# Moving turned softmax squares inside SBUF with twelve small DMAs instead of through DRAM, with a key ring whose last half is repeated

## The chip, the cores and the metric

The kernel runs on one core of a Trainium2 chip. The metric is the device time of one execution in microseconds, as the median over several runs. Beside it there is one profiled execution, whose trace gives the views that this document reads.

## The reference

Input x has 2 batches of 2048 tokens with 128 features, all in float32. There are three parts, with layer norms and residual additions between them. The whole is computed as follows:

```
y = norm(x);  x += softmax(y y^T over the first token axis) y        # once, 2048 x 2048 per batch
twice:
    s = norm(x)
    for each of 2 layers:                                             # 8 heads of 64, window 64
        h = half of the features of s shifted by one token
        q, k, v = h @ wqkv;  q, k = rotate(l2norm(q)), rotate(l2norm(k))
        p = softmax of q k^T over the own window of 64 keys and the one before
        s = s + (p v) @ wo
        s = s + (a * gelu(g)) @ w2,   a, g = norm(shifted s) @ w1     # hidden 341
    x += s
    after the first of the two: x += a token-wise weighting of norm(x)
```

The part that matters here is the windowed attention. For a query u of a group of 32 queries, the keys that count are 96 keys in three squares of 32: the weights of a group and head are a 32 x 96 matrix. To multiply the weights with the values, they must be turned so that keys lie on partitions.

## The kernel before

The kernel keeps activations transposed, features on partitions and tokens along the row. Tokens are cut into blocks of 128 (`NBLK` = 16 per batch) and chunks of 512. The first attention is one stage per batch (`first_attention`, L439 on). After it come four passes (two repetitions of two batches), each of 16 blocks through two layers: layer 1 runs `LAG` = 6 blocks behind layer 0, and the end of one pass runs beside the start of the next. In all there are 128 calls of `Attention.block`, which begins near L543.

The order of the work is not written by hand. Each step is declared with `op(engine, cost, fn, r, w, claim, late)`; `Program.run` is a list scheduler that knows each step's cost and the time until its result can be used (`TAIL`, `tail`), gives out buffers from pools (`slots`), and takes on each engine the ready step with the smallest number plus `late`. A step may start only if its buffers are free and the steps ahead of it can still be given theirs (`room`). What comes out is a fixed order on each of the five queues: TensorE (PE), VectorE (DVE), ScalarE (ACT), GpSimd (POOL) and SyncE (SP), which issues all DMAs. Each queue runs strictly in that order.

One block of windowed attention takes these steps, with the lines of the profile:

- A DMA fetches the rotation table (L551). TensorE projects q and k (L559, two steps) and v (L566); ScalarE squares (L582) and copies v (L567); two DMAs shift v by 64 partitions (L569, L573).
- VectorE multiplies with the table (L583, L584), reduces the squares (L587), and with a small matmul (L588) and POOL's products (L591, L597) q and k are normalised.
- VectorE turns q (L606) and k (L607). The turned keys go to `kring`, a ring of `R` = 3 slots of 128 keys per layer.
- TensorE computes the scores (L628), with masks added by matmuls (L637). `keys(a)` says where the 96 keys of a group of 32 queries lie in the ring; on slot 0 the keys of the block before are at the ring's other end, so groups 0 and 1 take two pieces.
- VectorE takes the maximum (L649), ScalarE the exponentials (L654), VectorE the sum and its reciprocal (L660, L661), POOL multiplies (L666).
- VectorE turns the weights in squares of 32 x 32 (L677) into `xp`. Four DMAs write the rows of `xp` to a DRAM buffer `far`, one for each group (L686), and one DMA reads the whole back as `pT` with all four groups beside each other (L691). The parts of `far` that no square covers were set to zero once, by 32 DMAs (L520).
- TensorE combines values and weights (L702), ScalarE copies the result (L709), and every second block TensorE applies `wo` (L715). Every fourth block is followed by the feed-forward part (L751, L767, L776).

Buffers of 128 x 1024 floats come from the pool `w`. At the start it is empty: its 18 parts are first the buffers of the first attention and turn into `w` when that has done with them. `xn0` and `xnT0` are free when batch 0 has passed the first attention, the others when batch 1 has.

## Time and profile before

| what | value |
|---|---|
| median of 3 runs | 1640.41 us (1636.79 to 1644.73) |
| the profiled execution | 1623.37 us, of which its span is 1621.3 us |
| granted TensorE clock, mean | 0.96 |
| busy: PE, DVE, POOL, ACT | 91%, 83%, 66%, 59% of the span |
| DMAs issued by SP | 1164 |
| moved by the DMA engines | 208.55 MB |

A busy share counts the time in which at least one instruction of the engine ran. PEld is TensorE's loading of weights, which runs beside its matmuls. SP counts no busy time: its instructions issue DMAs or wait. In the rows, `out<-in` names the tile written and the tile read; `far` is the DRAM buffer, while `arena` and `right` are the memory from which the pool `w` is made.

### The profile page before, as it was taken

Reading aid. Unit: us, or ns where it says so; the run is one execution under the profiler, and the core shown is the slowest. Engines: PE = TensorE matmul, PEld = TensorE weight load, DVE = VectorE, ACT = ScalarE, POOL = GpSimd, SP = SyncE. Lnnn points to the kernel's source line nnn. Section 1 sums busy time; section 2 is a strip of 40 time slices with the busy share of each in tenths; the row PEclk is TensorE's granted clock in tenths of the full one; section 3 lists DMA queues with packets and bytes.
Section 4 is the critical chain, followed back from the end, with each engine's and each line's share of the span. In section 5 each row is a group of like instructions: output and inputs, shape, how many; then the busy total and the mean of one; then the engine's idle time right before and its main releaser. Section 6 shows DMA issues by size and latency. Waiting matters only on the chain.

```text
span 1621.3 us, 53049 instructions
## 1 busy us (share of the span) xinstructions
PE 1482.7 (91%) x21659; PEld 844.0 (52%) x21659; DVE 1341.4 (83%) x2464; ACT 960.0 (59%) x2426; POOL 1072.2 (66%) x1308
## 2 busy tenths in 40 slices
PE   7999997989999999699999899799999999899875
PEld 4454554545555555355555464455555555555543
DVE  4533378799999899989998999989999989899772
ACT  6453455566666566465666666556666756566652
POOL 3440147578697767758687757758697877786561
PEclk9999998999999999799999999789999999999997
DMA  5540025455464543235555443255555555555432
GB/s 191 163 148 1 14 67 142 111 150 156 136 172 124 156 134 97 84 98 167 144 144 164 118 137 105 58 153 152 147 153 169 154 147 157 139 152 153 133 97 60
DMA packets 183542, 208.55 MB, mean 129 GB/s; under 512 B 18474, under 2 KB 143876, under 8 KB 183300
## 3 DMA queue, kind: packets, MB, share of 16 engines
q1 hardware_dynamic: 183300, 205.18, 44.4%
q8 instruction: 170, 2.79, 0.7%
q14 instruction: 72, 0.59, 0.1%
HBM read 111.78 MB, written 61.87 MB: 107 GB/s over the span
## 4 chain that ended last, share of the span: by engine, by line
PE 60%; DVE 17%; DMA 9%; POOL 5%; issue 4%; SPq 2%; ACT 2%; POOLq 0%; DVEq 0%; ACTq 0%
PE pp L751 9%; PE pp L559 9%; PE pp L702 6%; PE pp L628 6%; PE pp L715 5%; PE pp L468 5%; PE pp L566 5%; PE pp L776 4%; DMA arena<-far 3%; PE pp L482 2%; PE pp L479 2%; PE pp L460 2%; DMA right<-far 2%; DVE b_m L660 2%; DMA far<-arena 2%
## 5 line engine op out<-in xcount | busy, mean ns | idle before, releaser
L559 PE MATMUL pp<-wqkv,b_s 128*32 128x256 f32 x4096 | 263.4, 389 | 3.3 <-DVE arena L584 1.6
L654 ACT ACTIVATE arena<-pp,b_m 128x96 f32<-128x96 f32 x776 | 198.6, 363 | 92.2 <-DVE b_m L649 88.8
L666 POOL TENSOR_TENSOR arena<-arena,b_m 128x384 f32<-128x384 f32 x194 | 156.5, 827 | 91.1 <-DVE b_m L661 47.7
L751 PE MATMUL pp<-b_c,w 128*128 128x512 f32 (+1 forms) x384 | 176.8, 609 | 10.0 <-POOL b_c L747 7.8
L559 PEld LDWEIGHTS pp<-wqkv,b_s 128*32 128x32 f32 x4096 | 115.9, 110 | 129.8 <-issue 29.8
L628 PE MATMUL pp<-kring,b_c 64*32 64x96 f32 (+2 forms) x9728 | 150.2, 245 | 17.5 <-DVE kring L607 8.9
L628 PEld LDWEIGHTS pp<-kring,b_c 64*32 64x32 f32 x9728 | 121.5, 109 | 76.2 <-issue 33.6
L597 POOL TENSOR_TENSOR arena<-arena,b_n 128x1024 f32<-128x1024 f32 x80 | 152.9, 1913 | 3.5
L649 DVE TENSOR_REDUCE b_m<-pp 128x4 f32<-128x384 f32 x256 | 131.2, 540 | 18.8 <-PE pp L637 17.5
L566 PE MATMUL pp<-wqkv,b_s 128*128 128x512 f32 x256 | 143.8, 650 | 2.6 <-DVE b_n L589 2.6
L591 POOL TENSOR_TENSOR arena<-arena 128x1024 f32<-128x1024 f32 x51 | 120.9, 2370 | 36.4 <-DVE arena L584 28.5
L582 ACT ACTIVATE arena<-pp 128x512 f32<-128x512 f32 x170 | 100.9, 605 | 57.7 <-PE pp L559 49.9
L751 PEld LDWEIGHTS pp<-b_c,w 128*128 128x128 f32 (+1 forms) x384 | 67.3, 181 | 104.4 <-issue 72.4
L702 PE MATMUL pp<-arena,b_v 128*64 128x64 f32 x2560 | 96.1, 230 | 25.0 <-DMA arena<-far 14.1
L702 PEld LDWEIGHTS pp<-arena,b_v 128*64 128x64 f32 x2560 | 85.3, 143 | 61.0 <-issue 34.0
L584 DVE TENSOR_TENSOR arena<-pp,b_tab 128x512 f32<-128x512 f32 x172 | 114.0, 673 | 0.2
L583 DVE TENSOR_TENSOR arena<-pp,b_tab 128x512 f32<-128x512 f32 x160 | 105.7, 671 | 9.2 <-ACT arena L582 6.3
L567 ACT COPY b_v<-pp 128x512 f32<-128x512 f32 x128 | 75.7, 594 | 54.0 <-PE pp L566 53.8
L587 DVE TENSOR_REDUCE b_n<-arena 128x32 f32<-128x1024 f32 x85 | 101.8, 1198 | 1.7 <-ACT arena L582 1.7
L709 ACT COPY arena<-pp 128x512 f32<-128x512 f32 x80 | 47.6, 595 | 84.0 <-PE pp L702 82.0
L660 DVE TENSOR_REDUCE b_m<-arena 128x8 f32<-128x768 f32 x97 | 90.5, 933 | 7.3 <-ACT arena L654 6.9
L597 POOL TENSOR_TENSOR right<-right,b_n 128x1024 f32<-128x1024 f32 x48 | 92.3, 1923 | 2.3
(213 smaller groups left out, 3390.5 us busy)
## 6 DMA issues: line engine op xcount, KB each, us to landing
arena<-far SPq DMA_DIRECT2D x80, 512.0 KB, 4.2
far<-arena SPq DMA_DIRECT2D x344, 96.0 KB, 1.9
b_tab<-turn SPq DMA_DIRECT2D x128, 256.0 KB, 3.0
b_v<-b_v SPq DMA_DIRECT2D x248, 128.0 KB, 2.6
right<-far SPq DMA_DIRECT2D x48, 512.0 KB, 4.1
far<-right SPq DMA_DIRECT2D x168, 96.0 KB, 2.5
turn<-b_tab SPq DMA_DIRECT2D x32, 256.0 KB, 2.0
b_tab<-in_rot_dram SPq DMA_DIRECT2D x16, 256.0 KB, 2.8
```

The lines of the kernel that those rows point to most:

```text
L559: pe_.matmul(out=pq[k]()[c * 32 : c * 32 + 32, a * 256 : (a + 1) * 256], lhsT=s()[:, at : at + 32], rhs=wqkv[:, l, c * 256 : (c + 1) * 256 ...
L566: op("PE", 0.885, lambda: pe_.matmul(out=pv(), lhsT=h(), rhs=wqkv[:, l, 2 * INNER : 3 * INNER], start=True, stop=True), r=keys_of(s, q) + ...
L584: op("DVE", dve(512), lambda part3=part3, src=src, trig=trig: dv.tensor_tensor(part3(t2), src(), trig(1), ALU.mult), r=[pq[k], tab], w=[(t ...
L591: op("POOL", pool(1024), lambda: po_.tensor_tensor(halves(t1), halves(t1), halves(t2)[:, :, ::-1, :], ALU.add), r=[t2], w=[t1], late=47)
L597: lambda: po_.tensor_tensor(t1().rearrange("p (h d) -> p h d", d=32), t1().rearrange("p (h d) -> p h d", d=32), nr()[:, 0:32].unsqueeze(2) ...
L628: pe_.matmul(out=sim[par]()[a * 32 : a * 32 + 32, pair * 96 + c0 : pair * 96 + c0 + n], lhsT=qT()[rows, pair * P + a * 32 : pair * P + a * ...
L649: op("DVE", dve(384), lambda sim3=sim3, mx=mx: dv.tensor_reduce(mx(), sim3(), AX.X, ALU.max, negate=True), r=[sim[par]], w=[(nm, par)])
L654: ac.activation(p()[:, hd * 96 : (hd + 1) * 96], sim[par]()[:, k * 96 : (k + 1) * 96], AF.Exp, bias=nm()[:, hd : hd + 1])
L660: op("DVE", dve(768), lambda: dv.tensor_reduce(rs()[:, 0:HEADS], p3(), AX.X, ALU.add), r=[p], w=[rs])
L666: lambda hs=hs: po_.tensor_tensor(p3()[:, hs, :], p3()[:, hs, :], rs()[:, hs].unsqueeze(2).to_broadcast([P, 4, 96]), ALU.mult),
L702: pe_.matmul(out=av()[par * 64 : par * 64 + 64, pair * P + w * WIN : pair * P + (w + 1) * WIN].rearrange("p (a c) -> p a c", a=2), lhsT=(v ...
L751: op("PE", pe(512), lambda: pe_.matmul(out=p_()[0:n, :], lhsT=w1[:, l, off + j * P : off + j * P + n], rhs=d(), start=True, stop=True), r= ...
```

## The change

The squares of the turned weights go from `xp` to `pT` within SBUF: for each of the four groups and each of the three squares one DMA of 32 partitions with 256 floats each, twelve a block, in place of four writes to `far` and one read. `far`, its zeroing DMAs and the constant for them are gone; the uncovered parts of `pT` are zeroed by four memsets on POOL when batch 0's first attention has ended. For this, `pT` has a pool of its own with four buffers, made of `xn0` and `xnT0`, which no longer go to `w`.

The key ring gets 64 more columns in front. When a block has written slot 2, a DMA copies the second half of that slot into them, so that slot 0 finds the keys before it without a break; only the first block of a pass still uses two pieces.

Other pools change in size: `c` 12 to 10, `s1` 3 to 2, `n` 7 to 10, `m` 12 to 18, `row` 4 to 8. The scheduler's figures change: the tail of a DMA from 2.0 to 2.6, the cost of the scores from 1.02 to 1.14 (1.26 for a first block), and nearly every `late` number. So the order on all five queues is a new one. The diff without the `late` numbers:

```diff
-    kring = [fixed([P, 4, R * P], f"kring{l}") for l in range(DEPTH)]
+    kring = [fixed([P, 4, WIN + R * P], f"kring{l}") for l in range(DEPTH)]
...
-    slots["far"] = [scratch.tile([4 * P, 256], F32, name=f"far{i}") for i in range(8)]
+    slots["pT"] = []
...
-        "xn0": [("w", part[4]), ("w", part[5])],
+        "xn0": [("pT", part[4]), ("pT", part[5])],
...
-        "xnT0": [("w", part[8]), ("w", part[9])],
+        "xnT0": [("pT", part[8]), ("pT", part[9])],
...
+        if not b:
+
+            for x in (xn, xnT):
+                for odd in range(2):
+                    z0 = 0 if odd else 96
+                    op("POOL", 1.1, lambda x=x, odd=odd, z0=z0: po_.memset(x()[z0 : z0 + 32, :].rearrange("p (n a c) -> p n a c", n=2, a=4)[:, :, odd::2], 0.0), w=[x])
...
-    def clear():
-        for far in slots["far"]:
-            for a in range(4):
-                z0 = a * P + (0 if a % 2 else 96)
-                op("SP", 0.4, lambda far=far, z0=z0: sp.dma_start(out=far[z0 : z0 + 32, :], in_=I["zero"]), w=[(nought, z0)], late=7)
...
+            if slot == R - 1:
+                op("SP", 0.4, lambda: sp.dma_start(out=ring[:, :, 0:WIN], in_=ring[:, :, R * P : WIN + R * P]), r=[(ring_, slot)], w=[(ring_, "before")], tail=3.0)
...
-                at, own = slot * P + 32 * a - WIN, WIN - 32 * a
+                at, own = slot * P + 32 * a, WIN - 32 * a
                 if own > 0 and first:
-                    return (0, slot * P, own), (own, slot * P, 96 - own)
-                if own > 0 and not slot:
-                    return (0, prev * P + P - own, own), (own, 0, 96 - own)
+                    return (0, WIN + slot * P, own), (own, WIN + slot * P, 96 - own)
                 return ((0, at, 96),)
...
-            xp, pT, far = buf("w"), buf("w"), buf("far")
+            xp, pT = buf("w"), buf("pT")
...
             for a in range(4):
-                op(
-                    "SP", 0.4,
-                    lambda a=a, z0=a * P + 32 * (a % 2): sp.dma_start(
-                        out=far()[z0 : z0 + 96, :].rearrange("(n k) c -> k n c", k=32), in_=xp()[a * 32 : a * 32 + 32, 0:768].rearrange("k (n c) -> k n c", n=3)
-                    ),
-                    r=[xp, nought], w=[(far, a)], tail=3.2, late=85,
-                )
-            op("SP", 0.4, lambda: sp.dma_start(out=pT().rearrange("p (a c) -> p a c", a=4), in_=far().rearrange("(a p) c -> p a c", a=4)), r=[far], w=[pT], tail=3.6, late=40)
+                for n in range(3):
+                    z0 = 32 * (a % 2 + n)
+                    op(
+                        "SP", 0.37,
+                        lambda a=a, n=n, z0=z0: sp.dma_start(out=pT()[z0 : z0 + 32, a * 256 : (a + 1) * 256], in_=xp()[a * 32 : a * 32 + 32, n * 256 : (n + 1) * 256]),
+                        r=[xp], w=[(pT, 3 * a + n)], tail=2.2,
+                    )
```

## The prediction

> **What bounds the kernel now.** I read the page first (engines, slices, chain), then the busy time by stretch, then the score, DMA and wait rows that the change touches.
>
> ```profile
> PE 1482.7 (91%) x21659; PEld 844.0 (52%) x21659; DVE 1341.4 (83%) x2464; ACT 960.0 (59%) x2426; POOL 1072.2 (66%) x1308
> ...
> PE 60%; DVE 17%; DMA 9%; POOL 5%; issue 4%; SPq 2%; ACT 2%; POOLq 0%; DVEq 0%; ACTq 0%
> ```
>
> TensorE holds 60% of the chain that ended last, VectorE 17%. But shares of the whole span mix stages, so I cut it where the first projection of an attention block runs (193.8 us) and where the planner's ramp is over:
>
> ```profile
> 100.00:194.00 94.00, 94.00 (x314) 47.83 (x316) 28.39 (x83) 39.92 (x95) 11.62 (x14) 1.00 0.09 33
> 194.00:221.00 27.00, 27.00 (x272) 14.57 (x265) 20.61 (x41) 13.19 (x29) 12.85 (x14) 1.00 0.23 59
> 221.00:273.00 52.00, 43.78 (x718) 23.95 (x716) 43.42 (x82) 27.86 (x80) 33.14 (x39) 0.95 0.40 107
> ...
> 400.00:650.00 250.00, 239.19 (x3905) 139.03 (x3905) 235.90 (x424) 161.02 (x401) 187.68 (x227) 0.99 0.50 140
> 1060.00:1500.00 440.00, 418.32 (x7319) 243.41 (x7319) 409.73 (x740) 286.15 (x743) 333.38 (x404) 0.98 0.54 152
> ```
>
> The columns after the length are PE, PEld, DVE, ACT, POOL busy. Up to 194 us TensorE is alone at 100% and VectorE at 30%. From 400 us on both are full: PE 95 to 96%, DVE 93 to 94%. So the blocks are bound by two engines at once, and time is gained only if both have less to do or wait less; VectorE has no work to lose in this change.
>
> **Part 1, fewer score matmuls.** With the last half of the key ring repeated in front of it, blocks on slot 0 need no second piece of keys, except the first block of a pass. Slot 0 comes 6 times in 16 blocks, 48 of 128 blocks; 8 of them are first blocks, so 40 change, each losing 16 matmuls. The timeline has both kinds:
>
> ```profile
> 1137.70 1.24 PE L628 MATMUL pp<-kring,b_c 64*32 64x64 f32 x90
> ...
> 1139.06 1.15 PE L702 MATMUL pp<-right,b_v 128*64 128x64 f32 x32
> ...
> 1188.57 0.93 PE L628 MATMUL pp<-kring,b_c 64*32 64x96 f32 x60
> ...
> 1189.60 1.12 PE L479 MATMUL pp<-b_s,meanw 128*128 128x512 f32 x2
> ```
>
> From the first score to the next step: 1.36 us with two pieces, 1.03 us with one. 40 x 0.33 = 13 us of TensorE work go. TensorE has 60% of the chain and VectorE is as full, so I book 8 us of the 13. The 40 added ring copies (one DMA each) follow a transpose whose readers come one block of the same layer later, two block times of 10.6 us (1356 us from 194 to 1550 us over 128 blocks); 3 us of landing fit in. If SP is held up for over 15 us there, the scores wait.
>
> **Part 2, the way of the squares.** The rows of before:
>
> ```profile
> L686 SPq DMA_DIRECT2D far<-arena x344: 302/433/1545, 239.3 to 1587.3; - x172
> L691 SPq DMA_DIRECT2D arena<-far x80: 371/382/1512, 244.2 to 1589.3; - x80
> L573 SPq DMA_DIRECT2D b_v<-b_v x120: 461/590/1724, 198.0 to 1547.4; - x120
> ...
> far<-arena SPq DMA_DIRECT2D x344, 96.0 KB, 1.9
> b_v<-b_v SPq DMA_DIRECT2D x248, 128.0 KB, 2.6
> arena<-far SPq DMA_DIRECT2D x80, 512.0 KB, 4.2
> ```
>
> Issue on SP takes 0.43 us for one of the four writes (0.48 from start to start), and these land 2.1 us later by the median of their line; the read back takes 4.2 us. The path is 3 x 0.48 + 2.1 + 0.2 + 4.2 = 7.9 us a block. No row is an SBUF-to-SBUF DMA of 32 rows of 1 KB. Its issue is bounded by 0.30 (the shortest L686) and 0.64 us from start to start (L573 right behind L569, 0.59 and the gap); I take 0.48, the row with the same kilobyte rows. Landing is bounded by 1.8 and 2.6 us (L569, SBUF to SBUF but four times the bytes); I take 2.1. New path: 11 x 0.48 + 2.1 = 7.4 us, bounds 5.1 to 9.6.
>
> Two rules of the Trainium skill are weighed here. L686 with four writes in 2 us shows that issues follow each other without waiting for landings. "SBUF — State Buffer", The DMA setup-cost knee, says each DMA pays some 2 us whatever its size, and that small ones should be joined; paid one after another this would be 12 x 2 = 24 us a block, a chain of 6.8 + 24 = 31 us against a cover of 17 (both below), and the sum would gain some 14 us on each of 128 blocks. The rows decide: the cost overlaps, and what counts is SP's 0.48. The same page, Door 1: The DMA port swizzle, says that 32 partitions reach 8 of 16 ports, an estimated 0.15 us for 32 KB at its 218 GB/s asymptote; that is below the issue spacing and is left out. Second, "DMA: Bandwidth & Descriptors", Anatomy of one DMA, calls the receipt of a write to HBM the heaviest, so SBUF should land sooner than the far write. The rows show the reverse order, 2.6 against 1.9 us; by the rule the path is at most 7.4 us, by the SBUF row 7.9. Neither changes the sign.
>
> SP's load: before, per block, 4 x 0.48 + 0.43 + 0.42 (table) + 1.15 (two value shifts) = 3.9 us, plus the stops of the queue until the far writes land:
>
> ```profile
> SPq L691 <- DMA far<-arena: 66.1, 71, 4.2
> ```
>
> With the 33.7 us of the same wait on the far writes from the other buffers, 99.8 us of stopped queue go. After: 12 x 0.48 + 0.42 + 1.15 + 0.15 = 7.5 us of every 10.6, 71%. In the changed kernel's order on SP, 64 of the 128 batches of twelve stand alone and the other 64 stand back to back with another batch; the second of a pair may start up to 5.8 us late, and table loads and value shifts queue behind both. In that order each small DMA also waits for the semaphore of the DMA eight before it; at 2.1 us landing and 0.48 spacing only some five are in flight, so this wait ends early; it decides from a landing of 3.8 us.
>
> What covers this path is the TensorE work that the planner put between the scores of a block and its combine. I took both kernels' orders and priced each step by its spacing in the trace (projection half 0.97, values 0.95, combine 1.08, output 1.83, feed-forward 0.89 each and 2.68). Mean cover: before 19.5 us (lowest tenth 15.0), after 16.9 (11.7). What it must cover: first maximum 0.54, eight exponentials 2.9, sum 0.93, reciprocal 0.18, two products 1.65, last transpose 0.56, then the path: 6.8 + 7.9 = 14.7 before, 14.2 after. Adding up the shortfall over all blocks at 14 gives 46 us before; the page's idle time before L702 is 25.0 + 17.6 = 42.6, so the sum is usable. In the middle (TensorE work 300 to 1300 us): before 13.8 us of shortfall at 14; after 7.3 if its chain is 13.5, 28.2 at 15, 55.4 at 16. For the pairs of batches I take 15: +14 us, bounds -7 and +42. At the end of the kernel the shortfall also grows (from 18.5 at 14 us to 48.9 at 15) but the work missing there was done earlier, so I book nothing.
>
> **Part 3, buffers.** Two of the early buffers (xn0, xnT0) now hold pT alone, so the general pool has nothing until the second batch's first attention frees its own. In the order before, the first projection stands 43 us of TensorE work ahead of the last first-attention matmul; after, 6 us. Before, VectorE did 20.6 us in 194 to 221 us, 15.7 of it for blocks by its lines; after, the first projection stands at 208 us of TensorE work, where before it stood at 181 and ran at 194, so it starts at about 221 us. Against that, 5.5 us of first-attention work on VectorE then lies behind it. So VectorE is 10.2 us behind in the stage where it is 93% busy: +11 us. Bounds: 5 (TensorE is free to serve it faster) and 15. If the cover of first-attention matmuls is gone, TensorE idles there; that is the form in which it will show. Four memsets on POOL, an estimated 1.0 us each from the 64x512 one's 0.52, lie where POOL is 12% busy: nothing. The 32 zeroing DMAs (0.59 us each at 35 to 69 us) go from SP, under 100% TensorE: nothing. If POOL or SP were late there, the tables would be, which are read after 194 us.
>
> **Part 4, waits on the engines.** Twelve landings mean more waiting instructions: on TensorE 1021 for 385, 781 of them at the combine for 161; on VectorE 549 for 404. At 51 ns each the 636 on TensorE would be 32 us at most, 7 us on VectorE. Before, a combine with 0, 1 or 2 of them follows an L559 matmul by 522 ns in each case, so they hide behind the matmul ahead; inside a combine one stretched the spacing from 34 to 51 ns. I take 2 us; the cover would fail if three in a row outlast the queue. Moving the remaining steps (new order numbers everywhere) I price at nothing: counts are the same and at each 100 us of TensorE work the VectorE work issued agrees within 5 us.
>
> **Sum.** -8 + 14 + 11 + 2 = +19 us against the profiled execution, which took 1623.4 us with what lies around its span of 1621.3: 1.2%. That execution is 1% below the median of the runs, so I carry the ratio over: 1640.4 x 1.012 = 1659 us.
>
> **Rivals.** Faster (0.26): the removed waits pay and the rest is hidden. L702's waits for the far reads are worth 24.6 us (14.1 + 10.5) on TensorE; half of them go, all 13 us of scores count, and the late start costs its 5: -13 - 12 + 5 = -20, 1620 us. For it: 9% of the chain is DMA, SP is stopped 100 us, the DMA engines lose 512 of 896 rows a block. Against: the planner has spent the shorter path on a thinner cover. It decides from an issue spacing below 0.37 us, where the path falls under 6.2 us and the pairs cost under 4.4.
>
> SP becomes the bound (0.15): at 0.64 us spacing a block costs 9.4 us of SP in 10.6, waits pass from queue to combine (+42 us and more at a chain over 16), and table loads come late: 1690 to 1740 us. Against: L686 shows 0.48.
>
> No change (0.14): early start and scores cancel, stalls in the middle stay as they are: 1640. That the ring does not spare the matmuls is excluded: the order after has 640 fewer.
>
> **Numbers.** About 0.5% (8 us) is what a measurement of this kernel can tell. My case, slower by up to 2.5%, has 0.45; with SP as the bound 0.60 for slower. The range takes in the bounds (-13 + 5 - 7 = -15 to -5 + 15 + 42 + 15 = +67) and part of the faster case: 1614 to 1707 us.
>
> **What would show it.** Right: L628 near 137 us busy instead of 150, first projection near 221 us, TensorE idle 10 us more before 300 us, SP's issues 0.48 apart, waits of the combine for DMA not smaller. Wrong: small DMAs at 0.35 us, PE idle before the combine well under 40 us, or scores waiting for the ring copy.

## The result: 1937 us, and the profile after

The changed kernel takes 1937.24 us (median of 4 runs, 1929.41 to 1939.72); the kernel before, in the same comparison, took 1639.43 us. The ratio is 1.1804, with a 95% interval of 1.1756 to 1.1851. The direction was forecast, the size was not: 298 us instead of 19, far above the range.

First the page of the changed kernel: the engines, and the two rows of the chain that ended last.

```profile
span 1937.9 us, 52332 instructions
...
PE 1596.3 (82%) x20379; PEld 896.4 (46%) x20379; DVE 1341.8 (69%) x2464; ACT 970.9 (50%) x2426; POOL 1076.8 (56%) x1312
...
PE 37%; SPq 28%; DVE 18%; DMA 8%; issue 5%; POOL 2%; ACT 2%; DVEq 0%; POOLq 0%; ACTq 0%
SPq L687 27%; PE pp L467 6%; PE pp L700 5%; DMA arena<-arena 4%; PE pp L749 4%; PE pp L557 4%; PE pp L459 4%; PE pp L564 3%; PE pp L627 2%; PE pp L713 2%; DVE b_m L648 2%; PE pp L774 2%; DMA arena<-right 2%; DVE b_n L585 2%; DVE arena L676 2%
```

No engine is full now. SP's queue had 2% of the chain before; it has 28%, nearly all in line L687, the twelve small DMAs. The trace has 1280 fewer matmuls of TensorE than before (21659; it shows two records for each of the 640 that the new order spares), and yet TensorE is busy 114 us longer. The stretches tell why (columns as before: length, then busy PE, PEld, DVE, ACT, POOL with counts, the granted clock, the DMA share, GB/s):

```profile
194.00:221.00 27.00, 25.93 (x101) 14.17 (x102) 12.70 (x30) 11.51 (x20) 5.25 (x5) 1.00 0.00 1
221.00:273.00 52.00, 42.85 (x637) 22.27 (x635) 43.37 (x79) 24.54 (x68) 29.98 (x33) 0.87 0.21 55
400.00:650.00 250.00, 206.54 (x3050) 117.09 (x3047) 183.33 (x330) 128.47 (x328) 154.00 (x187) 0.90 0.30 79
1060.00:1500.00 440.00, 363.44 (x5092) 205.91 (x5091) 341.81 (x610) 235.66 (x586) 274.54 (x340) 0.91 0.28 74
```

In the middle TensorE is busy 83% (before 95 to 96%) and VectorE 73 to 78% (before 93 to 94%), and the granted clock is 0.90 to 0.91 instead of 0.98 to 0.99. So the loss has two layers: the engines stand, and the matmuls that run take longer. It also runs through all stages; it is no matter of the start.

Now the rows that answer to L686 and to its wait. The first are the answer for line L687 (ns min/median/max, first and last start), then the two landings of the page, then the waits of TensorE (us in total, times, longest), those of the kernel before (L702) last:

```profile
L687 SPq DMA_DIRECT2D arena<-arena x996: 507/589/1967, 257.2 to 1905.0; - x200
L687 SPq DMA_DIRECT2D arena<-right x540: 507/589/2047, 278.5 to 1897.4; - x180
...
arena<-arena SPq DMA_DIRECT2D x996, 32.0 KB, 1.8
...
arena<-right SPq DMA_DIRECT2D x540, 32.0 KB, 1.8
...
PE pp L700 <- DMA arena<-arena: 169.3, 81, 4.4
...
PE pp L700 <- DMA arena<-right: 76.2, 35, 3.7
...
PE pp L702 <- DMA arena<-far: 14.1, 11, 3.1
PE pp L702 <- DMA right<-far: 10.5, 9, 3.9
```

One small DMA holds SP for 0.59 us; from start to start it is 0.633 us by the median in the trace (0.68 us by the mean). Twelve are 7.6 us of issues, and by these medians a batch has landed after 11 x 0.633 + 1.84 = 8.8 us. Landing, 1.84 us by the median, is no slower than the 2.1 us forecast. The combine (L700) now waits 245.5 us for these DMAs; before, its waits for the far reads were 24.6 us. SP's timeline in the middle of the kernel (start, length, what) shows the queue:

```profile
905.39 8.35 SPq L687 DMA_DIRECT2D arena<-right  x12
913.84 0.54 SPq L571 DMA_DIRECT2D b_v<-b_v  x1
914.48 0.54 SPq L567 DMA_DIRECT2D b_v<-b_v  x1
915.11 0.54 SPq L549 DMA_DIRECT2D b_tab<-turn  x1
915.74 8.07 SPq L687 DMA_DIRECT2D arena<-arena  x12
923.91 0.54 SPq L571 DMA_DIRECT2D b_v<-b_v  x1
924.55 9.25 SPq L687 DMA_DIRECT2D arena<-right  x12
```

In this stretch SP waits for nothing. It is not so everywhere: from 300 to 1500 us SP issues for 78% of the time (in the kernel before 39%) and waits in the rest for the steps that its next DMA needs. Everything that an attention block needs from memory goes through this one queue, the rotation tables (L549) and the value shifts (L567, L571) too, so they stand between batches of 8 to 9 us. VectorE now waits for tables, which it does for 1.1 us in all in the kernel `none` below, the same without the small DMAs:

```profile
DVE arena L582 <- DMA b_tab<-turn: 27.7, 7, 11.5
DVE right L582 <- DMA b_tab<-turn: 26.7, 5, 10.7
```

### The profile page after: what moved, and what is told of

Same layout as the page of the kernel before. It is cut to its first block, busy times and chain, and to the rows that moved or that the text cites. A ratio compares the mean times of both kernels' runs of the same rounds, so it can differ in the third digit from the quotient of the medians.

```text
span 1937.9 us, 52332 instructions
## 1 busy us (share of the span) xinstructions
PE 1596.3 (82%) x20379; PEld 896.4 (46%) x20379; DVE 1341.8 (69%) x2464; ACT 970.9 (50%) x2426; POOL 1076.8 (56%) x1312
## 4 chain that ended last, share of the span: by engine, by line
PE 37%; SPq 28%; DVE 18%; DMA 8%; issue 5%; POOL 2%; ACT 2%; DVEq 0%; POOLq 0%; ACTq 0%
SPq L687 27%; PE pp L467 6%; PE pp L700 5%; DMA arena<-arena 4%; PE pp L749 4%; PE pp L557 4%; PE pp L459 4%; PE pp L564 3%; PE pp L627 2%; PE pp L713 2%; DVE b_m L648 2%; PE pp L774 2%; DMA arena<-right 2%; DVE b_n L585 2%; DVE arena L676 2%
## 5 line engine op out<-in xcount | busy, mean ns | idle before, releaser
L700 PE MATMUL pp<-arena,b_v 128*64 128x64 f32 x4096 | 202.8, 254 | 250.3 <-DMA arena<-arena 169.3
L700 PEld LDWEIGHTS pp<-arena,b_v 128*64 128x64 f32 x4096 | 171.3, 162 | 320.5 <-issue 227.2
L665 POOL TENSOR_TENSOR arena<-arena,b_m 128x384 f32<-128x384 f32 x142 | 115.3, 831 | 97.6 <-DVE b_m L660 77.2
L653 ACT ACTIVATE arena<-pp,b_m 128x96 f32<-128x96 f32 x568 | 140.9, 365 | 54.3 <-DVE b_m L648 52.6
L627 PE MATMUL pp<-kring,b_c 64*32 64x96 f32 (+2 forms) x8448 | 142.0, 265 | 24.2 <-DVE kring L605 11.9
L653 ACT ACTIVATE right<-pp,b_m 128x96 f32<-128x96 f32 x456 | 113.3, 358 | 52.7 <-DVE b_m L648 47.6
L582 DVE TENSOR_TENSOR arena<-pp,b_tab 128x512 f32<-128x512 f32 x146 | 96.9, 676 | 56.6 <-DMA b_tab<-turn 27.7
L595 POOL TENSOR_TENSOR arena<-arena,b_n 128x1024 f32<-128x1024 f32 x68 | 130.1, 1913 | 2.5
L665 POOL TENSOR_TENSOR right<-right,b_m 128x384 f32<-128x384 f32 x114 | 92.5, 832 | 65.1 <-DVE b_m L660 46.1
L707 ACT COPY right<-pp 128x512 f32<-128x512 f32 x60 | 35.2, 586 | 183.0 <-PE pp L700 182.5
L589 POOL TENSOR_TENSOR right<-right,arena 128x1024 f32<-128x1024 f32 x34 | 80.3, 2361 | 56.2 <-DVE right L581 52.6
```

The lines of the kernel that those rows point to most:

```text
L582: op("DVE", dve(512), lambda part3=part3, src=src, trig=trig: dv.tensor_tensor(part3(t2), src(), trig(1), ALU.mult), r=[pq[k], tab], w=[(t ...
L595: lambda: po_.tensor_tensor(t1().rearrange("p (h d) -> p h d", d=32), t1().rearrange("p (h d) -> p h d", d=32), nr()[:, 0:32].unsqueeze(2) ...
L627: pe_.matmul(out=sim[par]()[a * 32 : a * 32 + 32, pair * 96 + c0 : pair * 96 + c0 + n], lhsT=qT()[rows, pair * P + a * 32 : pair * P + a * ...
L653: ac.activation(p()[:, hd * 96 : (hd + 1) * 96], sim[par]()[:, k * 96 : (k + 1) * 96], AF.Exp, bias=nm()[:, hd : hd + 1])
L665: lambda hs=hs: po_.tensor_tensor(p3()[:, hs, :], p3()[:, hs, :], rs()[:, hs].unsqueeze(2).to_broadcast([P, 4, 96]), ALU.mult),
L700: pe_.matmul(out=av()[par * 64 : par * 64 + 64, pair * P + w * WIN : pair * P + (w + 1) * WIN].rearrange("p (a c) -> p a c", a=2), lhsT=(v ...
```

## The experiments

Unless it is said otherwise, an experiment has the order and the buffers of the changed kernel, and each time is a median of 4 or 5 runs (narrow: one run; c11: 20). Ratios are to the kernel before, run beside it. Its medians there lie between 1633 and 1643 us, so a difference of under some 10 us between two experiments that were not run beside each other says nothing.

### Was it the order, the work, or the number of small DMAs?

**plan63.** The scheduler is told the measured price, so that the order is planned anew.

```diff
-                        "SP", 0.37,
+                        "SP", 0.633,
```

> The changed kernel, where the planner is told the measured 0.633 us for each of the twelve DMAs instead of 0.37; nothing else. Theory A (the order is wrong: a batch takes 7.6 us on SP where the planner reckoned with 4.4, so TensorE meets each combine some 3 us early and stands still there): the combines are placed later, idle time of TensorE at the combine falls from 250 us to under 80, and the time to 1640 to 1740 us. Theory B (capacity: SP has 9.6 us of issues for every block and cannot serve more blocks, however they are ordered): 1850 us or more, and the waits move elsewhere. Theory C (it is not SP: late start, smaller pools, more waiting instructions): 1900 to 1970 us.

**four.** Of the twelve DMAs only those of the first square of each group are issued; `eight` below issues two of three.

```diff
-  lambda a=a, n=n, z0=z0: sp.dma_start(...)
+  lambda a=a, n=n, z0=z0: (sp.dma_start(...) if n == 0 else None)
```

> The changed kernel with its order kept, but only four of the twelve DMAs of a block are issued, those of the first square of each group; the other squares are left out, so weights of two thirds of the keys are stale. Theories A and B: SP has 4.5 us per block and a batch takes 2.5 us; the time falls to 1620 to 1690 us, what is over 1640 being the price of late start, pools and order. Theory C: the time stays over 1850 us.

plan63 took 1994.42 us, ratio 1.2179 (1.2136 to 1.2222), slower than the changed kernel. Of the three theories only B has room for it (1850 us or more, the waits elsewhere). Its combine waits less for the squares, but the loss has moved to the tables:

```profile
PE pp L700 <- DMA arena<-arena: 56.4, 30, 4.1
PE pp L700 <- DMA arena<-right: 56.0, 32, 3.7
...
DVE arena L582 <- DMA b_tab<-turn: 69.4, 11, 15.8
```

So correcting the cost in the plan wins nothing back. four took 1569.1 us, ratio 0.9578 (0.9547 to 0.9608): with a third of the DMAs, everything else in the change is there and the kernel is 4% faster than before, below the 1620 to 1690 us expected.

**eight** and **narrow** ask for the dose and for the bytes; narrow moves 64 floats a row instead of 256.

```diff
- out=pT()[z0 : z0 + 32, a * 256 : (a + 1) * 256], in_=xp()[a * 32 : a * 32 + 32, n * 256 : (n + 1) * 256]
+ out=pT()[z0 : z0 + 32, a * 256 : a * 256 + 64], in_=xp()[a * 32 : a * 32 + 32, n * 256 : n * 256 + 64]
```

> The changed kernel with its order kept, but eight of the twelve DMAs issued (two squares of each group; the third is left out, so weights of a third of the keys are stale). SP has 7 us per block. If the loss grows evenly with each DMA, half-way between four (1569) and twelve (1937): 1750 us. If it starts only when a batch outlasts the 4.4 us that the order was made for (eight take 5.1), near 1600 us.

> The changed kernel with its order kept, all twelve DMAs issued, each with 64 floats a row instead of 256 (three quarters of each square are left out, so those weights are stale). If the 0.63 us are a price per DMA: spacing and time stay, 1900 to 1940 us. If they are the time of the bytes or of what the DMA engines can take: spacing under 0.4 us and time under 1650 us.

eight took 1655.61 us, ratio 1.0145 (1.0117 to 1.0173). From four to eight DMAs a block, each one more costs 22 us of the whole, from eight to twelve 70 us, so the loss does not grow evenly. narrow took 1893.29 us in its one run, just under the 1900 us expected of a price per DMA. Its issue is unchanged, so a quarter of the bytes takes little away and SP is paid per DMA:

```profile
L687 SPq DMA_DIRECT2D arena<-arena x996: 507/588/1799, 254.9 to 1859.0; - x200
```

### The same load laid on the kernel before

**before_plus8** puts two SBUF-to-SBUF DMAs of 32 rows behind each write to `far`, ahead of the read back, in the old order. **before_8behind** puts eight of 24 floats a row behind the read back, and nobody waits for them.

```diff
                 sp.dma_start(out=far()[z0 : z0 + 96, :]...)                        # before_plus8
+                for j in range(2):
+                    sp.dma_start(out=xp()[b : b + 32, c0 : c0 + P], in_=xp()[a * 32 : a * 32 + 32, j * P : (j + 1) * P])
...
                 sp.dma_start(out=pT()..., in_=far()...)                            # before_8behind
+                for a in range(4):
+                    for j in range(2):
+                        sp.dma_start(out=spare[b : b + 32, j * 24 : (j + 1) * 24], in_=ident[a * 32 : a * 32 + 32, j * 24 : (j + 1) * 24])
```

> The kernel before with its order kept; behind each of the four writes to the DRAM buffer SP issues two more DMAs of 32 partitions from xp into columns of xp that nobody reads, so twelve issues stand ahead of the read back. Theories A and B: 8 x 0.63 = 5 us more on SP in every block, met by a cover of 19.5 us over a chain of 14.7: the chain becomes 19.8, short in nearly half of the blocks, and SP stands at 9 us of 10.6; 1780 to 1950 us. Theory C: within 2% of 1640 us, since eight DMAs that nobody waits for cost only SP's time.

> The kernel before with its order kept; SP issues eight more DMAs of 32 partitions (24 floats a row, between tiles that nobody waits for) directly behind each read back, so the way of the squares itself is as long as before and only SP's time is taken. Theory B1 (SP's time: tables, value shifts and the next batch queue behind): 1800 us or more, near the 2102 of eight DMAs ahead of the read. Theory B2 (the length of the way from scores to combine): within 3% of 1640 us.

before_plus8 took 2102.07 us, ratio 1.2818 (1.2778 to 1.2858), beyond the 1780 to 1950 us expected; before_8behind 1890.01 us, ratio 1.1565 (1.1525 to 1.1604). The second is the cleaner one: SP's time, with no data wanted, costs the old kernel some 250 us. Its combine now waits 151.8 us for its own reads of `far` (before 24.6), which come late. No step reads `spare`, yet the trace puts some waits down to these DMAs too, which is not explained:

```profile
PE pp L710 <- DMA arena<-far: 101.3, 35, 6.6
PE pp L710 <- DMA right<-far: 50.5, 17, 4.9
...
PE pp L710 <- DMA spare<-ident: 34.1, 10, 6.0
```

Laid on the way of the squares, the eight DMAs, here of 128 floats a row and within `xp`, cost another 212 us. Not all of this is the way's length in DMAs: behind DMAs within SBUF the four writes to `far` themselves are issued more slowly, 0.58 us each by the median instead of the 0.43 us of the kernel before:

```profile
L684 SPq DMA_DIRECT2D far<-arena x344: 308/580/1819, 240.8 to 2060.0; - x172
```

So there are two costs, the queue's time and the length of the way, and the next three kernels separate them in the changed order.

### Spacing against waiting

**to_dram** sends the twelve DMAs to DRAM instead of to `pT`.

```diff
- sp.dma_start(out=pT()[z0 : z0 + 32, a * 256 : (a + 1) * 256], in_=...)
+ sp.dma_start(out=out_of(pT(), a, n), in_=...)        # 32 rows of a DRAM scratch, one scratch for each pT buffer
```

> The changed kernel with its order kept; the twelve DMAs go from the same rows of SBUF to a scratch in DRAM instead of to the rows that the combine reads (which stay at zero), so their data are left out, while the combine still waits for all twelve. It asks what sets the 0.63 us from one small DMA to the next, and tests the forecast at its own price. If SBUF on both sides sets it: spacing 0.43 to 0.50 us as for the writes to DRAM of the kernel before, a batch of twelve about 5.8 us, SP at 7.5 us a block, and the time that of about nine DMAs at 0.63 by the counts four, eight and twelve (1569, 1656, 1937): 1690 to 1740 us; by the forecast's sum 1659. If a DMA of 32 rows costs 0.63 us wherever it goes: spacing 0.60 to 0.65 us and 1900 to 1960 us.

One sentence of this expectation was wrong: the combine's matmuls read rows that no DMA writes, so they wait for none of the twelve. What was measured is the spacing alone: 1660.13 us, ratio 1.0153 (1.0117 to 1.019). The issue is short again, 0.464 us from start to start, with landings of 1.6 us:

```profile
L696 SPq DMA_DIRECT2D far<-arena x996: 302/419/1988, 256.6 to 1640.3; - x200
...
far<-arena SPq DMA_DIRECT2D x996, 32.0 KB, 1.6
```

The same source rows, the same 32 x 1 KB; only the destination differs. So it is the destination in SBUF that makes 0.633 us of 0.464; whether that is the memory, or that the rows lie on 32 partitions there and one behind the other in the scratch, is not shown. That 1660 agrees with the forecast of 1659 is chance, since the wait is missing. The next two complete the table: **dram_waits** sends the last of the twelve to `pT`, so that the combine waits for the end of a batch; **nobody** keeps SBUF to SBUF, with 24 floats a row, into a spare tile that nobody reads.

```diff
- out=out_of(pT(), a, n)                                                                     # dram_waits
+ out=pT()[z0 : z0 + 32, a * 256 : (a + 1) * 256] if 3 * a + n == 11 else out_of(pT(), a, n)
...
- out=pT()[z0 : z0 + 32, a * 256 : (a + 1) * 256], in_=xp()[..., n * 256 : (n + 1) * 256]    # nobody
+ out=spare[z0 : z0 + 32, a * 24 : (a + 1) * 24], in_=xp()[..., n * 256 : n * 256 + 24]
```

> In the kernel to_dram no combine waited for a small DMA after all: its matmuls read rows that no DMA wrote. Here eleven of the twelve go to DRAM and the last one to the rows that the combine reads, so the combine waits for the end of the batch (eleven squares are left out). Spacing about 0.48 us on the mean (eleven of 0.46 and one of 0.63), the forecast's own figure, and the way 11 x 0.46 + 1.84 = 6.9 us. If the spacing is the only term of the forecast that failed: 1640 to 1700 us, and 15 to 60 us of waits for DMA at the combine. If waiting for the end of a batch costs by itself what the change lost: 1720 to 1850 us.

> The changed kernel with its order; the twelve small DMAs go from SBUF to a spare tile of SBUF, 24 floats a row, and no engine waits for them; their data are left out. Spacing 0.63 us, as with 64 floats a row, whose time was 1893 us. If SP's time alone is the cost (tables and value shifts late behind 7.6 us of issues): 1780 to 1870 us. If the cost is that the combine waits for the end of a batch of 8.8 us: near to_dram, 1650 to 1700 us.

dram_waits took 1742.2 us, ratio 1.0615 (1.0567 to 1.0663), and nobody 1807.79 us, ratio 1.1014 (1.0959 to 1.1068). In a table, in us:

| spacing of the small DMAs | no combine waits for them | the combine waits |
|---|---|---|
| 0.46 to 0.48 (to DRAM) | 1660 (to_dram) | 1742 (dram_waits) |
| 0.63 (within SBUF) | 1808 (nobody) | 1893 (narrow), 1937 (the changed kernel) |

Going down costs 148 us without the wait and 151 or 195 us with it; going right costs 82 us in the upper row, 85 or 129 in the lower. The columns are not quite alike, since dram_waits waits for the last of the twelve alone and narrow and the changed kernel for all. dram_waits met the expectation of a cost of waiting (1720 to 1850 us), nobody that of a cost of SP's time (1780 to 1870 us); neither alone is the whole. Where the two pay shows in their waits. First dram_waits, then nobody with the issue of its small DMAs; its combine waits for none of them, but its tables and ring copies come late behind them:

```profile
PE pp L709 <- DMA arena<-arena: 82.3, 43, 5.0
PE pp L709 <- DMA arena<-right: 39.6, 23, 4.8
...
L688 SPq DMA_DIRECT2D spare<-arena x996: 507/588/1806, 256.6 to 1800.6; - x200
...
DVE arena L583 <- DMA b_tab<-turn: 73.5, 8, 13.7
...
DVE right L583 <- DMA b_tab<-turn: 59.5, 9, 14.3
...
PE pp L628 <- DMA kring<-kring: 38.5, 8, 15.7
```

In to_dram and nobody the squares are still read from `xp`, whose buffer is free only when they have landed; in nobody waits for that, of ScalarE, GpSimd and VectorE, come to some 64 us in all, none of them at the combine.

### The floors of the two orders

**none** issues no small DMA at all; **before_none** leaves out the four writes and the read back of the kernel before, in its own order, and its combine reads the identity.

```diff
- sp.dma_start(out=pT()...)                                  # none
+ None
...
- sp.dma_start(out=far()...), sp.dma_start(out=pT()..., in_=far()...)   # before_none
+ None
- rhs=pT().rearrange("p (a c) -> p a c", a=4)[:, 2 * w : 2 * w + 2, at : at + 32]
+ rhs=ident[:, at % 64 : at % 64 + 64].rearrange("p (a c) -> p a c", a=2)
```

> The changed kernel with its order and none of the twelve small DMAs; the combine reads rows that stay at zero and waits for no square (the squares are left out). The floor of the changed order: 1540 to 1569 us (four small DMAs gave 1569). Beside before_none it gives the sum of the forecast's parts 1, 3 and 4 without part 2: -8 + 11 + 2 = +5 us by the forecast; if the late start costs nothing, 8 to 13 us less than before_none.

> The kernel before with its order, without the four writes and the read back of each block; the combine's matmuls, same in number and shape, read the identity instead and wait for no square (the squares are left out). The floor of the order before. By the forecast's parts 1, 3 and 4, 5 us less than none; by the matmuls that the repeated ring saves alone, 8 to 13 us more than none. If the two differ by over 25 us, the new order as such is better or worse than the old.

none took 1558.18 us, ratio 0.9514 (0.9452 to 0.9576), and before_none 1591.1 us, ratio 0.9726 (0.9674 to 0.9777). So the way over DRAM cost the old kernel 46 us, the small DMAs cost the new one 379 us, and apart from the way of the squares the changed kernel is 33 us the better. The rows of none to hold against the changed kernel's, and the combine's row in the changed kernel (first) and in none (busy us, mean ns, idle before it):

```profile
PE 1460.8 (94%) x20379; PEld 820.0 (53%) x20379; DVE 1329.5 (85%) x2464; ACT 961.2 (62%) x2426; POOL 1074.1 (69%) x1312
...
400.00:650.00 250.00, 238.17 (x3768) 135.64 (x3774) 239.28 (x431) 167.47 (x416) 197.29 (x243) 0.99 0.21 54
...
L700 PE MATMUL pp<-arena,b_v 128*64 128x64 f32 x4096 | 202.8, 254 | 250.3 <-DMA arena<-arena 169.3
...
L700 PE MATMUL pp<-arena,b_v 128*64 128x64 f32 x4096 | 151.9, 229 | 2.1 <-DVE b_n L587 0.8
```

The matmuls are the same 20379. With the small DMAs they are busy 1596.3 instead of 1460.8 us, 135 us more, at a mean granted clock of 0.90 instead of 0.977; and TensorE stands 1937.9 - 1596.3 = 342 us instead of 98. Thus of 379 us some 244 are standing and 135 slower matmuls. Of the 135, 51 are the combine's alone (202.8 against 151.9 us), whose matmuls are also drawn apart by the waits between them; the other 84 are spread over the other lines. For these the lower clock is the likely cause, and that it follows from the standing is an inference: in the kernels here the clock is lower where TensorE stands more, and the Trainium skill's page "TensorE: Matmul & The Clock Gate", Part 1, says that the gate follows how busy TensorE has just been.

### The order with the old way, and the ring by itself

**far_kept** keeps order and ring of the changed kernel and moves the squares by the old five DMAs, at the places of the twelve. **far_after** does the same with the zeroing and the buffers of before as well, and is planned anew.

```diff
- sp.dma_start(out=pT()[z0 : z0 + 32, ...], in_=xp()[...])
+ sp.dma_start(out=far[z0 : z0 + 96, :]..., in_=xp()[a * 32 : a * 32 + 32, 0:768]...)   # only where n == 0
+ sp.dma_start(out=pT()..., in_=far...)                                                 # only where a == 3 and n == 2
```

> The changed kernel, complete, with its own order and ring kept, but the squares go over DRAM as before: four writes and one read back a block, at the places of the twelve small DMAs. It asks whether the new order, whose floor is 33 us below that of the old one, beats the kernel before with the old way of the squares. If the number of small DMAs is what the change pays for: SP's issues fall from 7.6 to 2.4 us a block, the squares' way takes 4 x 0.48 + 2.1 + 4.2 = 8.2 us on a thinner cover, and its price lies between the 46 us of before and some 100 us: 1558 + 46 to 100 = 1604 to 1660 us. If the order was laid so thin that a way of 8 us cannot be covered, whatever SP does: 1690 us and more.

> The changed kernel with the squares part undone: four writes to the DRAM buffer and one read back, zeroing DMAs, pT from the general pool again. Ring, pool sizes and the new order numbers stay. If SP's twelve issues are the whole loss, this is at or under the kernel before: 1580 to 1650 us, the ring being worth up to 13 us, the rest the new numbers. If the new order or the smaller pools carry a part of the loss, 1680 us or more.

far_kept took 1714.03 us, ratio 1.0419 (1.0379 to 1.0459), and far_after 1692.48 us, ratio 1.0367 (1.0329 to 1.0404). The old way, 46 us in the old order, costs 1714 - 1558 = 156 us in the new one. SP issues little in far_kept, so this is the price of the thinner cover and of the places that the five DMAs have in this order:

```profile
PE pp L716 <- DMA arena<-far: 77.8, 39, 6.0
...
SPq L345 <- DMA far<-arena: 186.6, 126, 4.1
...
SPq L345 <- DMA far<-right: 102.3, 80, 4.1
```

The queue stands 289 us until the writes have landed, against 99.8 us before; the five DMAs follow each other here with nothing between them. The two causes are not told apart.

**ring_c11** is the kernel before with the repeated ring; the memory for it comes from one buffer less in pool `c`, and **c11** is the control with that buffer gone.

```diff
-        "w": (1024, 0), "c": (512, 12),
+        "w": (1024, 0), "c": (512, 11),
...
-    kring = [fixed([P, 4, R * P], f"kring{l}") for l in range(DEPTH)]    # ring_c11 only
+    kring = [fixed([P, 4, WIN + R * P], f"kring{l}") for l in range(DEPTH)]
```

> The kernel before with one buffer less in the pool c (12 to 11), control for the next one. The order is made anew. No more than 10 us off the kernel before: 1630 to 1650 us.

> The kernel before with the ring's last half repeated and pool c at 11; the squares go over DRAM as before, one DMA more every third block. Part 1 of the prediction alone: 8 to 13 us less than with c at 11, 1620 to 1640 us. If the ring copies hold up the queue or the scores, no gain or a loss of up to 15 us. The order is made anew, which alone may move the time by some 2%.

c11 took 1641.88 us, ratio 1.0043 (1.0023 to 1.0063), as expected, and ring_c11 1675.3 us, ratio 1.0261 (1.0214 to 1.0307), where at most 1655 us were expected. TensorE's busy time falls by the expected amount, 1497.1 to 1485.6 us, but its idle time grows by 36 us. ring_c11 is planned anew, so this does not show that the ring costs something; a new order can hide a gain of 11 us, but the 40 copies were not tested apart from it.

### Two ways to relieve the queue

**act_half** issues the six DMAs of groups 2 and 3 from ScalarE's queue. **four_copied** lets ScalarE copy the four squares that stay on their own partitions, and moves eight. Both are planned anew.

```diff
-                        "SP", 0.37,                                       # act_half
-                        lambda a=a, n=n, z0=z0: sp.dma_start(...)
+                        "ACT" if a >= 2 else "SP", 0.63,
+                        lambda a=a, n=n, z0=z0: (ac if a >= 2 else sp).dma_start(...)
...
+                    if z0 == 32 * a:                                      # four_copied
+                        op("ACT", act(256), lambda ...: ac.copy(pT()[z0 : z0 + 32, ...], xp()[a * 32 : a * 32 + 32, ...]), r=[xp], w=[(pT, 3 * a + n)])
+                        continue
```

> The changed kernel with the six DMAs of groups 2 and 3 issued by ScalarE's queue instead of SP's, planned at 0.63 us each on both. Theory A and B: SP's part of a batch is 3.8 us, SP has 5.8 us per block; ScalarE, 50% busy, takes 3.8 us more per block; 1640 to 1760 us. Theory C: over 1850 us. If ScalarE's own queue becomes the bound (exponentials behind DMA issues), 1760 to 1850 us with ScalarE's waits grown.

> The changed kernel, complete, with the four of the twelve squares that stay on their own partitions copied by ScalarE and eight moved by DMA. If the number of small DMAs on SP is what counts, about the 1656 us of the kernel with eight, plus what four copies a block (about 0.4 us each, 1.6 us of ScalarE's 10.6 us a block) put on the path: 1660 to 1720 us. If the squares' way as such is slow, whoever moves them, 1800 us and more.

act_half took 1820.95 us, ratio 1.1112 (1.1062 to 1.1162), within the 1760 to 1850 us expected if ScalarE's queue suffers, and four_copied 1753.75 us, ratio 1.0727 (1.069 to 1.0765), dearer than the 1660 to 1720 us expected; whether by the copies or by the new order is open. Both are better than the change and worse than before. On ScalarE's queue a small DMA costs about the same time, and waits of ScalarE's computing steps are now put down to it:

```profile
L687 ACTq DMA_DIRECT2D arena<-arena x432: 513/602/2124, 256.5 to 1783.0; - x144
...
ACT b_n L590 <- DMA arena<-arena: 47.8, 11, 8.6
ACT arena L653 <- DMA arena<-right: 47.8, 11, 7.4
```

"DMA: Bandwidth & Descriptors" of the Trainium skill, Issuing engines are not separate DMA queues, says that a second issuing engine saves only the sequencer's time, "which is usually small relative to the DMA itself". Here that time is 0.633 us against a landing of 1.84 us, and since the landings overlap and the issues do not, it is the larger of the two over a batch, 7.0 of 8.8 us. Sharing it out, in an order planned for it, saved 116 us against the changed kernel.

No kernel that moves all squares was faster than the kernel before. four and none are, but they leave squares out.

## Why the prediction was wrong, step by step

**The sum against what was measured.** The kernels above split the difference. The split belongs to this sequence of steps; another sequence would give shares some tens of us apart, as the table of two by two shows.

| step | forecast, us | measured, us | from |
|---|---|---|---|
| parts 1, 3, 4 and the new order | +5 | -33 | before_none 1591 to none 1558 |
| the way over DRAM taken away, twelve DMAs at 0.48 us put in (0.46 in the two kernels), with the wait | +14 | -46 + 102 + 82 = +138 | 1637 to 1591, none 1558 to to_dram 1660 to dram_waits 1742 |
| spacing 0.633 instead of 0.48, and the wait for all twelve | 0 | +195 | dram_waits 1742 to 1937 |
| sum | +19 | +300 | |

That the direction came out right rests on the way of the squares alone; the first row had the wrong sign.

**The spacing of the issues (taken 0.48, measured 0.633) is the step that failed most.** It cost 148 us without the combine's wait and 151 to 195 us with it. The bounds were right, 0.30 to 0.64, and so was the path, 8.8 us by medians within 5.1 to 9.6. The choice between them was wrong: the forecast took the row with rows of the same kilobyte, L686, which writes to DRAM. The upper bound came from L573, which moves within SBUF, and this is what counts: narrow shows that bytes do not matter, to_dram that the destination does. The fitting row was on the page.

**What a full queue costs was not in the sum at all.** SP's 7.5 us of each 10.6 were worked out, and it was said that tables and value shifts queue behind the batches, but that was priced at nothing. nobody and to_dram price it without any wait of the combine for a square: 250 us over none at 0.633 and 102 us at 0.464. Set against the pace of none (first projection at 227.2, last at 1503.0 us, so 10.0 us a block), the small DMAs and the 2.0 us of other issues (a table 0.58, two shifts 1.17, a third of a ring copy) fill SP like this:

| kernel | SP's issues a block, us | share of 10.0 us | over none, us |
|---|---|---|---|
| four | 2.5 + 2.0 | 45% | 11 |
| eight | 5.1 + 2.0 | 71% | 97 |
| to_dram (no wait) | 5.6 + 2.0 | 76% | 102 |
| dram_waits | 5.7 + 2.0 | 77% | 184 |
| nobody (no wait) | 7.6 + 2.0 | 96% | 250 |
| the changed kernel | 7.6 + 2.0 | 96% | 379 |

The shares are reckoned with medians. With the mean spacings (0.53 us in to_dram, 0.68 us in the changed kernel) to_dram comes to 83% and the last two rows to 102%, so these could not have kept the pace of none. At 45% the queue is nearly free. In to_dram it is not, though no combine waits for the small DMAs there and the queue is not yet the bound by its sum; where between the two the loss sets in is not measured without a wait. Work for several blocks shares the one queue in order, in lumps of twelve, so a table that is wanted early stands behind a batch that is wanted late.

**The cover at the combine (+14, bounds -7 to +42) had the right sign and the wrong size.** The forecast said that the new order has a thinner cover and that the planner had spent the shorter path on it. far_kept agrees: the same five DMAs cost 46 us in the old order and 156 in the new one, though part of the 156 is the queue's own waiting. Adding up shortfalls from both orders in units of fixed step times gave 46 for the old order, and before_none, which also frees SP, gained the same 46; but the same sum with a chain of 15 us gave far too little after. It assumed that squares start their way when their chain is done, apart from pairs of batches. In the changed kernel they start when the queue is free, by the timeline above 8 to 9 us later if another batch is ahead. The "up to 5.8 us late" of the forecast was worked out with 12 x 0.48.

**The rival with SP as the bound (0.15, 1690 to 1740 us) was the right mechanism at the right spacing and still too small.** It took 42 us and more for the cover, and the late tables as a small addition. The measured addition, 250 us in nobody, is larger than the 129 us that the combine's waits add to it. A bound read from the rows would have been SP's time a block against the pace, 9.4 of 10.6 us; so near to full, the forecast should have widened the range upward rather than kept it at +67.

**Part 1 was right in its matmuls.** The scores take 142.0 us busy, where 137 were forecast, but at the lower clock; in none, at 0.977, they take 134.3 against 150.6 in before_none, at 0.962, 16.3 us less for the 13 worked out (some 14 of them at an equal clock, an estimate from the two clocks). What they are worth in the whole is not shown by itself: the 33 us between the two kernels hold the new order too.

```profile
L627 PE MATMUL pp<-kring,b_c 64*32 64x96 f32 (+2 forms) x8448 | 142.0, 265 | 24.2 <-DVE kring L605 11.9
...
L627 PE MATMUL pp<-kring,b_c 64*32 64x96 f32 (+2 forms) x8448 | 134.3, 252 | 23.6 <-DVE kring L605 18.4
...
L628 PE MATMUL pp<-kring,b_c 64*32 64x96 f32 (+2 forms) x9728 | 150.6, 245 | 18.5 <-DVE kring L607 8.5
```

The rows are of the changed kernel, none and before_none. **Part 3** found the first projection at 227.2 us (forecast 221), but the price of +11 us is not to be seen in its place: in none, TensorE is busy 61.7 of the 73 us from 227 to 300, in before_none 61.0, and none is 33 us ahead at the end. **Part 4**, booked at 2 us, was not measured by itself. With 529 waiting instructions on TensorE where before had 385, four is 11 us over none in all. Of the 1021 of the changed kernel the combine, there 51 us longer busy than in none, has 781; but dram_waits, with 88 at its combine, is already 28 us longer busy there.

**The signs that were named.** Issues 0.48 apart: wrong, and the spacing alone told that the forecast had failed. The combine's waits for DMA not smaller: right, ten times as large. First projection and scores: right as said. TensorE idle 10 us more before 300 us: from 100 to 300 us it is idle 20.8 us after and 11.9 before, but that came true by luck. In none it is idle 13.0 us there, so 7.8 of the 8.9 us come from the small DMAs and not from the late start that the sign stood for. Scores waiting for the ring copy, a sign against the forecast, are 2.5 us in the changed kernel.

**The rules that were weighed.** "SBUF — State Buffer", The DMA setup-cost knee, was set aside because latencies overlap. They do: 1.84 us of landing, 0.633 from one to the next. Yet its advice to join small DMAs was right here, for the issue and not for the latency. "DMA: Bandwidth & Descriptors", Anatomy of one DMA, which describes DMAs issued by GpSimd, calls the receipt of a write to HBM the heaviest. For SP's DMAs of equal size the write to DRAM is not the slower to land: 1.57 us in to_dram, 1.84 us within SBUF. Of the 0.27 us between them 0.17 are the issue.

**What stays open.** Why a destination in SBUF takes SP 0.17 us longer per DMA, and why the write to `far` behind such a DMA does too (before_plus8), was not tried further. Which of parts 1, 3 and 4 and the new order makes the 33 us of none over before_none is not told apart. How the 195 us between dram_waits and the changed kernel divide between spacing and the more numerous waits of the combine (for all twelve DMAs instead of for the last) is open too; narrow's 1893 us, a single run with all twelve waits, puts some 44 us of it on the width of the rows.

## What to carry to other kernels

Price a DMA that is moved or multiplied by the issue time of a row with the same memories at both ends, not with the same bytes, and multiply by the count before looking at latency: eleven spacings of 0.633 us were 7.0 of the 8.8 us of the way. Then add up all issues of the queue for one turn of the loop and set the sum against the loop's pace. In this kernel a queue filled to 45% by medians cost 11 us and one filled to 76%, whose small DMAs no combine waited for, 102 us: what else stands in the in-order queue comes late, so the cost is not only in the wait of the reader but also in loads that have nothing to do with the change. When a change brings a new order with it, measure the order by itself first (both kernels with the disputed transfers left out), since here the order and the transfers had opposite signs.

## What the runs showed of the hardware

- SP's time for one DMA of 32 rows within SBUF was 0.633 us from start to start, by the median, the same with 1 KB, 256 bytes or 96 bytes a row (the changed kernel, narrow, nobody); to DRAM from the same rows it was 0.464 us (to_dram). On ScalarE's queue it was alike (0.60 us of issue, act_half).
- How long an issue takes depends on the DMA ahead of it in the queue too: the same write of 96 KB to `far` took at the least 0.30 us, 0.43 us by the median in the kernel before, where other such writes stand ahead of most, and 0.58 us in before_plus8, where two DMAs within SBUF do.
- The landing took 1.84 us within SBUF and 1.57 us to DRAM for the same 32 KB, from the start of the issue (0.59 and 0.42 us of it).
- The granted TensorE clock went with the share of the span that TensorE was busy: 0.977 at 94% busy (none), 0.954 at 89% (to_dram), 0.938 at 88% (far_kept), 0.92 at 84% (nobody), 0.90 at 82% (the changed kernel), 0.867 at 76% (before_plus8). If the clock follows the standing, as this order suggests, a stall costs more than its length: beside 244 us of standing the matmuls outside the combine took 84 us longer, the combine's own 51 us.
